# A four-layer graph network on one core: the maximum of layer 2 in one PSUM bank, narrower pieces for its count matrices, a bias row moved to layer 3, and more steps between the pieces of a node tile

## The chip, the cores and the metric

The kernel runs on one core of a Trainium2 chip. The metric is the time of one execution on the device in microseconds (us); less is better. The engines are named as the profile names them: PE (TensorE matmul), PEld (its weight loads), DVE (VectorE), ACT (ScalarE), POOL (GpSimd) and SP (SyncE, which here issues DMA transfers). PSUM is the memory that PE writes; its unit here is a bank of 128 partitions x 512 float32. SBUF is the working memory, DRAM the large one.

## What is computed

A graph of N = 6250 nodes (49 node tiles of 128) and E = 100000 edges, sorted by destination (782 edge tiles of 128). Node features are 256 wide, hidden ones 512 wide, float32. Low destinations have many more edges than high ones, because the destination is 6250 times the square of a uniform number.

```python
h = maximum(layernorm(x), 0)
h = h @ W1_self + mean_of_neighbours(h) @ W1_neigh + b1          # layer 1
hp = relu(h @ W2_pool + b2_pool)
h = h @ W2_self + max_of_neighbours(hp) @ W2_neigh + b2          # layer 2
h = ((sum_of_neighbours(h) + h) / (deg + 1)) @ W3_neigh + b3     # layer 3
h = h @ W4_self + mean_of_neighbours(h) @ W4_neigh + b4          # layer 4
out = x + h @ W_fc + b_fc
```

A node without edges has 0 for its maximum.

## The kernel before, in words

One function holds the fast path; a second, general path is run only if a flag (`bad`) says that the graph has not the expected form, which does not happen with these inputs. The kernel is written as loops that emit instructions for all engines; a scheduler then orders them on each engine by that order of emission and by what they depend on, and each engine runs its own instructions strictly in order. Work that is to lie beside a main loop is cut into generators (Python functions that `yield` between pieces); the main loop asks each for a piece at every step. So the number of `yield`s between two pieces sets how much of the main loop's work comes between them in the engines' queues.

**Sums over neighbours** (layers 1, 3 and 4) are done in two ways. For high destinations, gathered rows are multiplied on PE by one-hot matrices (`sums`, L382 on). For low destinations ("hubs", node tiles d below 18), a dense matrix A of edge counts is made per d (128 destinations by 49 x 128 sources) and multiplied on PE (`dense`, L469 on). Features go into these matmuls as three bf16 parts, high, middle and low (`parts`, L293 to L299: ACT copies the high part, DVE subtracts, ACT copies the middle one, DVE subtracts).

**Count matrices.** `build` (L309 on) makes A of tile d from windows of 8 destinations: 16 windows for each d. For each piece of a window ACT makes a one-hot of 128x128 in two steps (ht L319, hs L321), DVE one of 128x392 (hm L323: 49 source tiles x 8 destinations), PE multiplies them into a PSUM bank (pb L329), ACT reads that bank twice: once to find a count that is too large (many L337, with an accumulator, in `most`), once to copy it to A as fp8 (L339). SP stores A (tab_a) at the end of a d. A window of d = 8 and above has at most 256 edges, so two pieces. `Hub.advance` (L345 on) makes the one-hots `LOOK` = 4 pieces ahead of the matmul; ht has 3 buffers, hs and hm 7. Tiles d = 0 to 7 are made in layer 1, d = 8 to 17 during layer 2.

**Layer 2, the maximum** (main loop L1218 to L1292). The edges lie in six blocks of 52, 100, 220, 180, 130 and 100 tiles, each block one partition-major stretch of edges, taken from the last to the first. Each of the 782 steps is for one edge tile: POOL issues a gather of 128 rows of 2 KB (L1240) into a buffer of two steps (X2, 2 x 3 buffers), DVE takes the running maximum within a destination, `run = max(run * same, X)` (L1247), where `same` is 1 if this edge has the destination of the one before it on the partition, and 0 otherwise. For each pair of steps, one more instruction writes the maximum of both steps into the first row of the pair (L1283), and SP stores that (L1288). The running maximum goes to and fro between two PSUM banks (run0, run1 of the pool psr2).

**Beside the maximum** every step also advances: `products2` (weight products, first 64 steps), `hub` (count matrices of d = 8 to 17; d 8 to 15 by step 250, the rest after it, to step 682), `early` (below), the `carry` at the end of a block (L1113 to L1143: it joins the running maxima of the 128 partitions), and node tiles, `done2` (L1157 to L1196). `done2` of node tile d gathers the stored maxima (tot, L1149), joins them (L1164), transposes them on PE (L1168), copies them with ACT (hT L1170), multiplies with products of weights (L1173, L1176, L1179), adds the bias row prow with DVE (L1183), adds the result to layer 3's sum of that tile if d is below 16 (L1040), splits it in three parts and stores it (tab_r). From emission to end it takes about nine steps, and nothing but a count of tiles begun (49 in the steps from 112 to 762) sets when the next may start.

**Early products** (L1199 to L1215): for node tiles 6 to 37 layer 3's dense products start in layer 2, in batches of four source tiles: for each of the 16 destinations d, SP loads a piece of A (ae L1211), PE makes 3 matmuls for each source tile (pd L489), and the product is added to acc3[d] by DVE (`add3`, L1040) as soon as the last matmul has been emitted; the first addition of each d is a copy by ACT (L1043). Products use two PSUM banks (psd2). A share of 1/40 of the pieces left is emitted per step.

PSUM has eight banks of this kind; layer 2 has 3 for transposes and node tiles, 2 for early products, 1 for count matrices (psb2), 2 for the maximum.

**Prologue.** Edges of a window have to be found: `select`, `begins`, `row_begins`, `window_keys` (L656 to L770 or so) count for each window where it begins in the sorted list, in groups of 128 windows, 3 groups; `begins` gathers 128 rows of 782 destinations (drow L689, one buffer) and counts in them on DVE (L693).

## Time and profile before

| | |
|---|---|
| time, median of 3 runs | 3320.49 us (3316.07 to 3323.73) |
| the profiled execution: time | 3354.4 us |
| its span, first to last instruction | 3352.6 us |
| its mean granted TensorE clock | 0.885 |
| prologue and layer 1 | 0 to about 916 us |
| layer 2 | about 916 to 2345 us, of which the loop over edge tiles to about 2280 |
| layers 3 and 4 | about 2345 us to the end |

Durations below come from the profiled execution, which took 33.9 us longer than the median of the runs. A row of a group reads: line, engine, operation, output<-inputs with shapes, number of instructions, then busy us in all and mean ns of one, then idle time of that engine just before them with what ended it. A row of a view of waits reads: engine, what waited <- what it waited for, us in total, times, the longest. In a view by windows each engine has its busy us and (in brackets) the number of its instructions; then come the granted clock of TensorE, the share of the DMA engines that was busy, and the rate in GB/s.

### The profile page before, as it was taken

The page shows a single profiled execution, that of the slowest core. Times are in us where ns is not written, and L with a number is a line of the kernel's source. Part 1 is how long each engine was busy: PE and PEld are TensorE (multiplying, and loading weights), DVE is VectorE, ACT ScalarE, POOL GpSimd, SP SyncE. Part 2 cuts the span into 40 slices and gives each one's busy share as a digit, 9 for nine tenths or more (in the row PEclk, how much of TensorE's full clock was granted, in tenths as well). Part 3 has the DMA queues.
Part 4 walks back from the last instruction along what each step waited for, and adds up shares of the span by engine and source line. Part 5 has one row for each costly group of instructions (what it writes and reads, how often), then busy time and mean ns, then how long its engine had stood idle before and what let it go on. Part 6 is the DMA issues. An engine that isn't in the chain of part 4 may idle for free.

```text
span 3352.6 us, 39513 instructions
## 1 busy us (share of the span) xinstructions
PE 2515.0 (75%) x11395; PEld 1293.9 (39%) x11523; DVE 2178.8 (65%) x5588; ACT 993.2 (30%) x2703; POOL 1948.2 (58%) x2255
## 2 busy tenths in 40 slices
PE   4557888889776555588888923872889999888887
PEld 2134556556443222233333411331333333444444
DVE  7845555655378778677777886785456656355555
ACT  4845555553256787322111110000000001000000
POOL 4266656666455555555565666563666665566664
PEclk9678989999887676789989966986999999999999
DMA  5455656666688788788888888886999998666675
GB/s 175 150 150 150 171 168 178 180 189 181 193 276 260 251 266 280 257 282 270 277 282 277 285 283 263 268 280 208 366 325 328 340 323 298 214 197 198 202 205 170
DMA packets 350368, 806.06 MB, mean 240 GB/s; under 512 B 55694, under 2 KB 147318, under 8 KB 350108
## 3 DMA queue, kind: packets, MB, share of 16 engines
q0 software_dynamic: 146080, 513.65, 50.2%
q1 hardware_dynamic: 145976, 234.34, 19.2%
q10 hardware_dynamic: 58084, 55.44, 5.4%
q8 instruction: 93, 1.52, 0.2%
q14 instruction: 135, 1.11, 0.1%
HBM read 604.85 MB, written 199.17 MB: 240 GB/s over the span
## 4 chain that ended last, share of the span: by engine, by line
PE 55%; issue 13%; DVE 11%; ACT 7%; DMA 7%; another core or an unknown queue 5%; POOL 3%; ACTq 0%; DVEq 0%; POOLq 0%; SPq 0%
PE pd L489 15%; PE pg L433 10%; PE pd L484 5%; DVE run L1247 3%; PE pd L485 3%; PE pb L329 3%; PE pm_prf L1179 3%; PE pm_hp L928 3%; PE pm_hp L931 2%; PE pm_w L263 2%; PE pm_prf L1173 2%; PE pg L428 2%; DVE X L1283 2%; ACT hs L321 2%
## 5 line engine op out<-in xcount | busy, mean ns | idle before, releaser
L1240 POOL DMA_INDIRECT X<-rows,srcIf x782 | 755.3, 966 | 565.8 <-issue 212.5
L411 POOL DMA_INDIRECT ring<-tab_h,srcT x474 | 452.5, 955 | 280.7 <-issue 99.0
L433 PE MATMUL pg<-ring,hot 128*128 128x512 bf16 (+2 forms) x2431 | 532.3, 329 | 82.8 <-issue 34.4
L1247 DVE SCALAR_TENSOR_TENSOR run<-run,samef,X 128x512 f32<-128x512 f32 x758 | 571.6, 754 | 34.1 <-DMA X<-rows,srcIf 11.5
L462 DVE SCALAR_TENSOR_TENSOR acc<-pg,M,acc 128x256 f32<-128x256 f32 (+2 forms) x694 | 356.4, 538 | 150.8 <-PE pg L433 48.5
L411 POOL DMA_INDIRECT ring<-tab_r,srcE x342 | 332.9, 973 | 194.4 <-issue 80.4
L329 PE MATMUL pb<-hm,hs 128*128 128x392 bf16 x781 | 262.5, 380 | 223.2 <-ACT A L339 96.4
L489 PE MATMUL pd<-r,ae 128*128 128x512 bf16 x1494 | 368.9, 395 | 66.7 <-DVE acc L1040 41.1
L411 POOL DMA_INDIRECT ring<-tab_s,srcE x314 | 301.4, 960 | 187.9 <-PE pg L429 68.6
L321 ACT ACTIVATE hs<-ht,onef 128x128 bf16<-128x128 bf16 x781 | 293.5, 397 | 348.5 <-PE pb L329 128.1
L433 PEld LDWEIGHTS <-hot 128*128 128x128 bf16 x2448 | 245.8, 101 | 328.5 <-issue 183.9
L407 DVE TENSOR_SCALAR hot<-iota_bf,keyE 128x128 bf16<-128x128 bf16 x656 | 159.6, 272 | 260.5 <-PE pg L429 101.9
L484 PE MATMUL pd<-zt,ac 128*128 128x512 bf16 x835 | 300.0, 388 | 25.9 <-issue 23.7
L1283 DVE SCALAR_TENSOR_TENSOR X<-X,samef,run 128x512 f32<-128x512 f32 x379 | 279.6, 738 | 0.0
L485 PE MATMUL pd<-zt,ac 128*128 128x256 bf16 x882 | 245.1, 278 | 29.3 <-issue 26.8
L489 PEld LDWEIGHTS <-ae 128*128 128x128 fp8e4 x1536 | 155.2, 101 | 288.5 <-issue 141.9
L489 PE MATMUL pd<-zt,ac 128*128 128x512 bf16 x797 | 229.2, 386 | 24.0 <-issue 14.7
L407 DVE TENSOR_SCALAR hot<-iota_bf,keyT 128x128 bf16<-128x128 bf16 x474 | 119.9, 265 | 169.8 <-PE pb L329 51.5
L489 PE MATMUL pd<-Z,A 128*128 128x256 bf16 (+1 forms) x1176 | 195.2, 282 | 26.5 <-issue 10.1
L329 PEld LDWEIGHTS <-hs 128*128 128x128 bf16 x781 | 82.3, 106 | 286.3 <-issue 207.1
L1179 PE MATMUL pm_prf<-unf,hTf 128*128 128x512 f32 x392 | 189.0, 608 | 4.5 <-issue 4.4
L323 DVE TENSOR_SCALAR hm<-iota_w,mk 128x392 bf16<-128x392 f16 x461 | 150.0, 340 | 53.2 <-PE pb L329 23.9
(329 smaller groups left out, 3559.7 us busy)
## 6 DMA issues: line engine op xcount, KB each, us to landing
rows<-X SPq DMA_DIRECT2D x385, 256.0 KB
tab_r<-r SPq DMA_DIRECT2D x49, 384.0 KB
tab_a<-A SPq DMA_DIRECT2D x18, 784.0 KB
tab_t<-th SPq DMA_DIRECT2D x49, 256.0 KB
rows<-hpf SPq DMA_DIRECT2D x49, 256.0 KB
th<-tab_t ACTq DMA_DIRECT2D x49, 256.0 KB
X<-rows,srcIf POOLq DMA_INDIRECT x782
ac<-tab_a ACTq DMA_DIRECT2D x90, 112.0 KB
```

Of the source, the lines that this page charges most:

```text
L321: nc.scalar.activation(hots[0], t, AF.Relu, bias=one, scale=-1.0)
L329: nc.tensor.matmul(hold[0], hots[0], hots[1], start=(k == 0), stop=(k == k_of[w] - 1))
L411: nc.gpsimd.indirect_dma_start(out=ring[:, j % deep, :], out_offset=None, in_=table, in_offset=bass.IndirectOffsetOnAxis(ap=srcT[:, j - jb ...
L433: nc.tensor.matmul(pg[:, : F + c], hot[j], X[:, part * F : (part + 1) * F + c], start=(k == 0 and part == 2), stop=(k == n - 1 and part == 1),
L462: nc.vector.scalar_tensor_tensor(acc[d], half, m, acc[d], op0=ALU.mult, op1=ALU.add)
L484: nc.tensor.matmul(hold[0], a, z[:, : 2 * F], start=(s == ss[0]), stop=False)
L485: nc.tensor.matmul(hold[0][:, :F], a, z[:, 2 * F :], start=False, stop=(s == ss[-1]))
L489: nc.tensor.matmul(hold[0][:, : F + c], a, z[:, part * F : (part + 1) * F + c], start=(s == ss[0] and part == 2), stop=(s == ss[-1] and pa ...
L1179: nc.tensor.matmul(pm, hT[:, c, :], un[:, c, :], start=False, stop=(c == KH - 1))
L1240: nc.gpsimd.indirect_dma_start(out=X[:, k, :], out_offset=None, in_=tab_p, in_offset=bass.IndirectOffsetOnAxis(ap=srcI[:, t : t + 1], axis=0),
L1247: nc.vector.scalar_tensor_tensor(run, prev, same[:, t : t + 1], X[:, k, :], op0=ALU.mult, op1=ALU.max,)
L1283: nc.vector.scalar_tensor_tensor(X[:, 0, :], X[:, 1, :], same[:, t : t + 1], before, op0=ALU.mult, op1=ALU.max,)
```

## The change

1. Count matrices of d = 8 and above (new function `build_narrow`): windows of 4 destinations instead of 8 (`WIN2`), 32 for each d, and one piece for each (at most 128 edges). The number of matmuls and of hm stays at 320; hm and the matmul are 196 wide instead of 392. Two pieces share a PSUM bank, ACT copies both at once, and that copy is emitted one pair later (`copies`). hs is made for four pieces at a time (128x512). hm has 16 buffers, hs 5 of four pieces, and the look ahead is 12 pieces. There are two banks (psb2). The check of counts reads A in SBUF in four "looks" per d, at up to 128x1664, in place of one read of PSUM per window. A has two buffers.
2. The running maximum stays in one PSUM bank, in place: first `run` with the pair's first row, then the pair's maximum into that row of X from the second row and `run`, then `run` with the second row. Number and width of the instructions stay.
3. The bias row of layer 2 leaves `done2` (49 additions of 128x512 on DVE, L1183) and goes into `qrow`, which layer 3 adds anyway; this holds because layer 3 divides the sum of deg + 1 equal rows by deg + 1. ACT now copies the high part from PSUM, and the first subtraction and `add3` read PSUM.
4. `done2` has about 21 steps instead of nine: 6 instead of 4 before the maximum, one before and one after the transposed copy, three after the matmuls, two after the high part, two after the middle one. A tile starts 11 steps after the last at the earliest. `carry` and `node_rows` have more steps too; `carry` gathers before it transposes.
5. The sum of an early product is not emitted at its end but just before the last piece of the next product (`take_sums`). Early pieces go at 1/32 of what is left per step.
6. The prologue has 4 groups of windows instead of 3: one `select`, one `begins` (a gather into the one drow buffer, and a count on DVE) and one column in each of the small tiles more.

The diff, cut to its core:

```diff
-WIN = 8
+WIN, WIN2 = 8, 4
...
+    def build_narrow(d, keys, pool, psb, copies):
...
+            def hot(r=r, v=v):
+                i = v % 4
+                if i == 0:
+                    held["ht"] = pool.tile([P, 4, P], BF16, name="ht", bufs=2)
+                nc.scalar.activation(held["ht"][:, i, :], iota_b, AF.Abs, bias=sk[:, r : r + 1])
+                hm = pool.tile([P, NT * WIN2], BF16, name="hm", bufs=16)
+                nc.vector.tensor_scalar(hm, iota_w[:, : NT * WIN2], mk[:, r : r + 1], None,
+                                        op0=ALU.is_equal)
+                held["hm", v] = hm
+                if i == 3:
+                    hs = pool.tile([P, 4, P], BF16, name="hs", bufs=5)
+                    nc.scalar.activation(hs, held["ht"], AF.Relu, bias=one, scale=-1.0)
+                    held["hs", v // 4] = hs
...
+                nc.tensor.matmul(pb[:, i * NT : (i + 1) * NT, :].rearrange("p s c -> p (s c)"),
+                                 held["hs", v // 4][:, v % 4, :], held.pop(("hm", v)),
+                                 start=True, stop=True)
...
+                def look(n):
+                    s0, s1 = LOOKS[n]
+                    at = NW1 + len(LOOKS) * (d - H1) + n
+                    many = pool.tile([P, 13, P], BF16, name="many", bufs=1)
+                    nc.scalar.activation(many[:, : s1 - s0, :], A[:, s0:s1, :], AF.Relu,
+                                         bias=less, accum_out=most[:, at : at + 1])
+
+                if i == 1:
+                    for f in copies[:2]:
+                        f()
+                    del copies[:2]
+                    copies.insert(0, copy)
+                    if v == WT2 - 1:
+                        copies.extend(lambda n=n: look(n) for n in range(len(LOOKS)))
...
-        psb = late.enter_context(tc.tile_pool(name="psb2", bufs=1, space=PSUM))
+        psb = late.enter_context(tc.tile_pool(name="psb2", bufs=2, space=PSUM))
...
-            yield from bias_rows(psm, b3c, B4, qrow)
+            yield from bias_rows(psm, b3c, B4, qrow, b2r)
...
+            yield
+            yield
+            yield
+            r3 = early_pool[0].tile([P, 3 * FH], BF16, name="r3", bufs=2 * BATCH + 1)
+            hi, mid, lo = (r3[:, i * FH : (i + 1) * FH] for i in range(3))
+            nc.scalar.copy(hi, pm)
+            yield
+            yield
+            if d < H3:
+                add3(d, pm)
             pr = wk.tile([P, FH], F32, name="prf")
-            nc.vector.tensor_add(pr, pm, prow)
-            yield
-            if d < H3:
-                add3(d, pr)
-            r3 = early_pool[0].tile([P, 3 * FH], BF16, name="r3", bufs=2 * BATCH + 1)
-            parts(pr, FH, r3)
+            nc.vector.tensor_sub(pr, pm, hi)
+            yield
+            nc.scalar.copy(mid, pr)
+            yield
+            yield
+            nc.vector.tensor_sub(lo, pr, mid)
...
-                             lambda s: batch[s], FH, psd, lambda v, d=d: add3(d, v))
-                early.add([(load, work[0])] + work[1:])
+                             lambda s: batch[s], FH, psd, lambda v, d=d: summed.append((d, v)))
+
+                def then(w):
+                    take_sums()
+                    w()
+
+                early.add([(load, work[0])] + [lambda w=w, i=i: then(w) if i == len(work) - 2 else w()
+                                               for i, w in enumerate(work[1:])])
...
+            run = psr.tile([P, FH], F32, name="run")
...
+                    row, st = X[:, k, :], same[:, t : t + 1]
+                    if s0 + G2 >= tb:
+                        step(row, X[:, 0, :] if k else run, st, row)
+                        if k:
+                            stored(b, s0 // 2, X)
+                    elif k == 0 and s0:
+                        step(run, run, st, row)
+                    elif k:
+                        held = run if s0 else X[:, 0, :]
+                        if s0 == 0:
+                            step(run, held, st, row)
+                        step(X[:, 0, :], row, st, held)
+                        if s0:
+                            step(run, run, st, row)
+                        stored(b, s0 // 2, X[:, :1, :])
...
-                    early.advance(early.done + math.ceil(early.left() / 40))
+                    early.advance(early.done + math.ceil(early.left() / 32))
...
-                    if tiles and not ends and begun2 < NT * (at - FIRST_AT) / (T - 20 - FIRST_AT):
+                    if (tiles and not ends and at >= begun_at + 11
+                            and begun2 < NT * (at - FIRST_AT) / (T - 20 - FIRST_AT)):
+                        begun_at = at
```

188 lines of the change are left out of this document (104 added, 84 removed).

## The prediction

> **What bounds the kernel now.** I read the page's table of busy time first, then the windows by stage, then the waits of POOL and DVE inside layer 2, then the groups by line there.
>
> The page: span and busy time of each engine.
>
> ```profile
> span 3352.6 us, 39513 instructions
> PE 2515.0 (75%) x11395; PEld 1293.9 (39%) x11523; DVE 2178.8 (65%) x5588; ACT 993.2 (30%) x2703; POOL 1948.2 (58%) x2255
> ```
>
> No engine is full over the span, and the stages differ. Almost all of the change lies in layer 2, so the next view cuts that out (916 to 2345 us), then its stages, then one stretch of 20 us.
>
> ```profile
> core 0: us, PE busy (x) PEld busy (x) DVE busy (x) ACT busy (x) POOL busy (x), PEclk, DMA share, GB/s
> 916.00:2345.00 1429.00, 955.46 (x3174) 434.32 (x3216) 1097.03 (x2068) 470.04 (x1320) 814.12 (x845) 0.82 0.82 269
> 916.00:1060.00 144.00, 111.99 (x377) 59.83 (x376) 114.87 (x324) 77.98 (x221) 79.91 (x85) 0.93 0.85 277
> 1060.00:1460.00 400.00, 229.58 (x622) 97.45 (x624) 311.01 (x678) 271.48 (x826) 225.24 (x231) 0.72 0.81 264
> 1460.00:1970.00 510.00, 422.65 (x1534) 189.93 (x1561) 400.80 (x640) 98.81 (x239) 295.58 (x307) 0.92 0.85 277
> 1970.00:2280.00 310.00, 177.26 (x609) 80.40 (x620) 242.81 (x373) 19.95 (x33) 191.29 (x198) 0.79 0.85 274
> 2280.00:2345.00 65.00, 13.98 (x33) 6.72 (x35) 27.54 (x57) 1.82 (x3) 22.10 (x24) 0.58 0.55 185
> 1985.00:2005.00 20.00, 0.00 (x0) 0.00 (x0) 16.77 (x25) 0.00 (x0) 15.11 (x17) 0.50 0.94 311
> ```
>
> The loop over the 782 edge tiles runs from 916 to 2280, 1364 us, and a tail of 65 us follows. DVE works 1097.03 of 1429, so it is idle 332 us; by stage 29.1, 89.0, 109.2 and 67.2 us in the loop and 37.5 in the tail. The last row is a stretch where nothing runs but gathers and the maximum: 17 gathers in 20 us at 311 GB/s, DMA share 0.94. That is the most that this mix of transfers reaches here. Bytes of the loop: 144 x 277 + 400 x 264 + 510 x 277 + 310 x 274 = 372 MB. At 311 GB/s they take 1196 us: the loop can lose at most 1364 - 1196 = 168 us, whatever DVE does.
>
> Are the gathers late, or does DVE hold them up? The waits of POOL, which issues the gathers, in layer 2 (what was waited for, us in total, times, longest):
>
> ```profile
> POOL X L1240 <- DVE run L1247: 132.9, 60, 6.5
> POOL X L1240 <- DVE X L1283: 44.9, 22, 5.8
> POOL X L1240 <- DMA rows<-X: 40.7, 28, 9.5
> POOL X L1240 <- DVE hm L323: 35.5, 22, 7.9
> ```
>
> and the waits of DVE in the same window:
>
> ```profile
> DVE acc L1040 <- remote: 47.3, 14, 7.9
> DVE hm L323 <- remote: 29.6, 9, 8.8
> DVE prf L1183 <- remote: 27.8, 4, 11.0
> DVE hm L323 <- PE pb L329: 21.3, 22, 3.4
> ...
> DVE run L1247 <- DMA X<-rows,srcIf: 9.6, 13, 1.3
> ```
>
> DVE waits for gathered rows 9.6 us in all, POOL waits 132.9 + 44.9 + 35.5 = 213 us for slots that DVE frees. **DVE is the pace-maker.** It runs in order, so a hub piece (hm), an early sum (acc) or a node tile (prf) that waits for PE or ACT holds the maxima behind it. "remote" is a release whose sender the trace did not resolve; for these three consumers it can only be PE or what PE waits for.
>
> **The change part by part.** The groups of DVE in layer 2 by line (xcount, busy, mean ns, then idle ahead of them):
>
> ```profile
> L1247 DVE SCALAR_TENSOR_TENSOR run<-run,samef,X 128x512 f32<-128x512 f32 x755 | 569.3, 754 | 32.1 <-issue 9.6 <-DMA X<-rows,srcIf 9.6 <-DVE run L1247 2.4
> L1283 DVE SCALAR_TENSOR_TENSOR X<-X,samef,run 128x512 f32<-128x512 f32 x378 | 278.9, 738 | 0.0
> L323 DVE TENSOR_SCALAR hm<-iota_w,mkR 128x392 bf16<-128x392 f16 x313 | 100.7, 329 | 67.7 <-remote 29.6 <-PE pb L329 21.3 <-issue 10.0
> L1040 DVE TENSOR_TENSOR acc<-acc,pd 128x512 f32<-128x512 f32 x112 | 76.3, 681 | 66.4 <-remote 47.3 <-PE pd L489 16.5 <-issue 2.5
> L297 DVE TENSOR_TENSOR prf<-prf,r 128x512 f32<-128x512 f32 x49 | 33.8, 689 | 26.9 <-ACT r L296 15.9 <-ACT ht L319 7.7 <-ACT hs L321 3.1
> L1183 DVE TENSOR_TENSOR prf<-pm_prf,prowf 128x512 f32<-128x512 f32 x49 | 33.6, 686 | 59.9 <-remote 27.8 <-PE pm_prf L1179 13.1 <-issue 6.1
> L299 DVE TENSOR_TENSOR r<-prf,r 128x512 bf16<-128x512 f32 x49 | 33.6, 686 | 8.2 <-issue 7.1 <-ACT r L298 0.9
> ```
>
> those of ACT:
>
> ```profile
> L321 ACT ACTIVATE hs<-ht,onef 128x128 bf16<-128x128 bf16 x314 | 117.6, 402 | 183.1 <-PE pb L329 60.7 <-remote 48.6 <-PE pd L489 25.3
> ...
> L337 ACT ACTIVATE many<-pb,less 128x392 bf16<-128x392 f32 x159 | 93.1, 586 | 114.3 <-PE pb L329 62.9 <-issue 23.2 <-remote 20.4
> ...
> L337 ACT ACTIVATION_READ_ACCUMULATOR many<-pb,less 128x1 f32 x159 | 31.5, 198 | 0.0
> ...
> L296 ACT CAST r<-prf 128x512 bf16<-128x512 f32 x49 | 30.2, 615 | 162.5 <-DVE prf L1183 48.5 <-issue 45.4 <-DVE run L1247 35.0
> ```
>
> and one group of the whole page, of the same kind of instruction as hm:
>
> ```profile
> L407 DVE TENSOR_SCALAR hot<-iota_bf,keyT 128x128 bf16<-128x128 bf16 x474 | 119.9, 265 | 169.8 <-PE pb L329 51.5
> ```
>
> (1) Bias row. The 49 additions at L1183 go: 33.6 us of DVE. The bias joins a row that layer 3 adds in any case, so nothing comes back there.
>
> (2) Four-node pieces. There are still 320 hm, 196 wide instead of 392. It takes 265 ns at 128 columns and 329 at 392: 0.242 ns per column, so 265 + 68 x 0.242 = 281 ns. 320 x 48 ns = 15 us of DVE go. On ACT, hs falls from 320 of 402 ns to 80 of 128x512; the nearest row that wide is L296 with 615 ns: 129 becomes 49 us. PE's matmuls halve in width, which only frees PE.
>
> (3) The check (many) falls from 160 of 586 + 198 ns, 125 us of ACT, to 40 "looks" at up to 13 x 128 = 1664 columns. No row is that wide. From L321 (128 wide, 402) and L337 (392 wide, 586) comes 0.70 ns per column, so 402 + 1536 x 0.70 = 1.47 us, with the accumulator's read 1.67: 67 us. Bounds: nothing for a piece that ACT runs while DVE wants nothing of it, and 40 x 1.67 = 67 us if DVE waits behind every one; I take nothing, for ACT is busy 470 of 1429 us and falls to about 330. The Trainium skill's "ScalarE: Activation LUTs", section "What ACT_TABLE_LOAD costs", gives 280 ns + 0.833 ns per element for an ACTIVATE with a pointer bias: 1.67 us without the read, 75 us in all by its figures; the row at 392 (586 against 607) agrees within 4%. By it the sum stays the same.
>
> (4) One bank for the maximum. Instructions and widths of L1247 and L1283 stay; each maximum now reads and writes the same PSUM bank where before it went from one to the other. No row shows that. In SBUF, L1040 adds in place in 681 ns and L299 not in place in 686. I take nothing. Bounds: below, nothing, for each instruction does the same work; above, reading and writing that exclude each other and so double it, 0.754 us more for each of the 758 that do this. It is a rival below. The Trainium skill's "PSUM — Partial Sum Buffer", section "The four PSUM rules", speaks for caution: each bank is a separate physical SRAM, so a read and a write that lay in two memories now lie in one. It states no price, and no row here shows one. By it alone, the sum could lie anywhere in that rival's range.
>
> (5) Two banks for the hub, 16 hm buffers and a look of 12. This is what the freed bank is for. PE's own waits in layer 2:
>
> ```profile
> PE pb L329 <- ACT A L339: 89.7, 44, 9.0
> ...
> PE pd L489 <- DVE acc L1040: 41.1, 10, 8.7
> ```
>
> With one bank, PE waits for ACT's copy 89.7 us; hm buffers come free only when PE has read them, and DVE stands before hm 67.7 us. After the change, PE has a second bank and DVE runs twelve pieces ahead instead of four. I leave 20 us of the 67.7.
>
> (6) Steps between a node tile's pieces. DVE's idle time before L1183, L297 and L299 is 59.9 + 26.9 + 8.2 = 95 us: it is asked for the result as soon as PE or ACT is asked to make it. Now there are three steps between matmuls and the copy, two more before each subtraction, and tiles start at least 11 steps apart. A step is 1364/782 = 1.74 us, two steps 3.5, while one ACT copy takes 0.6. I leave 30. The cover is ACT's and PE's being on time; a stall of PE over about 5 us still shows.
>
> (7) Early sums are taken one product later, so PE is done long before: of 66.4 I leave 25. What is late next is PE, which may wait for DVE to free the product's bank (a rival). SP's loads of A pieces are issued where they were relative to their product; the maximum's store is issued one instruction earlier. Carry's extra steps spread the same instructions. Early pieces go at 1/32 instead of 1/40 of what is left per step; the total is unchanged.
>
> (8) The prologue makes one more group of window starts: one gather, one pass of 128x782 on DVE, one selection. Its gathers use one buffer and so come one after another:
>
> ```profile
> L689 POOL DMA_INDIRECT drow<-dflat,cI x3: 950/955/1102, 17.1 to 34.6; - x3
> ```
>
> Three from 17.1 to 34.6 is 8.75 us apart. Bounds: 0 (it is hidden behind other preparation) and 8.75; I take +5, as PE's first layer-1 work depends on other keys of that prologue only in part.
>
> **The sum.** DVE's work falls by 33.6 + 15 = 49 us, its waits by 48 + 65 + 41 = 154. DVE alone would then let the loop run in 1364 - 203 = 1161 us. That is under the 1196 that the bytes take at 311 GB/s, so from somewhere DMA takes over. I place the loop midway between its present 277 GB/s and the stretch's 311: 294 GB/s, 372/0.294 = 1265 us. So -99 in the loop, 0 in the tail (65 us, where only the last tile is unspread in both), +5 in the prologue: -94. The profiled execution took 3354.4 us, so 3260.4; it stood 33.9 over the median of the runs, 3320.49, and I subtract the same: **3226 us**, 2.8% faster.
>
> **The rivals.**
>
> A. Only the removed work counts. The stalls are PE's own ("remote" is over half of the waits of acc, and the clock falls to 0.72 in 1060 to 1460), and they move with the work. Then -49 + 5: 3320.5 - 44 = 3276 us. For it: three of the longest waits are over 7 us, longer than the added two or three steps. Against: hub and early sums get far more than three steps.
>
> B. DMA's ceiling is all that is left: -168 + 5, 3157 us. For it: DVE's own sum is below that. Against: all four stages of the loop have other transfers and pieces beside the gathers, and none exceeds 277.
>
> C. Nothing comes of it, the stalls go to other waits, 3314 to 3327. Against: 49 us of work on the pace-maker go in any case.
>
> D. **Slower:** PE waits for the late sums. There are 128 early products with two banks; the sum of one is issued only before the last piece of the next, behind what DVE has queued. PE's idle time while they run is (510 - 422.65) + (310 - 177.26) = 220 us, so it decides from 220/128 = 1.7 us per product; at 3 us, 128 x 3 - 220 = +164 of PE's own, less the 49 of DVE: 3320 + 115 = 3435. For it: PE already waits 41.1 us for exactly this add, 4 us a time. Against: DVE's work is 1097/782 = 1.4 us a step, so a sum issued a piece before it is needed is mostly done in time.
>
> E. **Slower:** the in-place maximum costs more. The forecast gain of 94 is used up at 94/758 = 0.124 us each, a mean of 878 ns at L1247. Doubled it is +572 - 94: 3798. For it only that no row shows it; against, in-place in SBUF is free.
>
> **How the numbers follow.** Forecast (3190 to 3260): 0.43. A (3260 to 3314): 0.24. B (3145 to 3190): 0.08. C: 0.05. D: 0.13, half of it between 3327 and 3350. E: 0.07. The range 3150 to 3350 leaves out half of D, E and the edge of B, some 0.15 to 0.18. A measurement of this kernel tells about 0.2%, 6.6 us, from no change. Faster by more than that: 0.43 + 0.24 + 0.08 = 0.75; within: 0.05; slower: 0.20.
>
> **What would show it.** Loop of layer 2 about 1265 us with 290 to 300 GB/s; DVE idle before hm near 20, before the tile's subtractions near 30, before the early sums near 25; L1247 still at 754 ns, hm at 281; no waits of pb for ACT's copy; waits of PE's products for acc not over about 100 us; ACT at about 330 us in layer 2; prologue later by 0 to 9 us. Wrong if L1247's mean rises, if "remote" waits of DVE remain over 80 us in all, if the loop's rate stays at 277 (then the removed waits have come back as others), or if PE's waits for acc grow to over 150 us.

## The result, and the profile after

The changed kernel takes 3314.47 us (median of 20 runs), the kernel before 3324.86 us (median of 20 runs beside them): a ratio of 0.9965, 95% interval 0.995 to 0.9979. So it is 0.35% faster, about 11 us where 94 were forecast. The profiled execution of the changed kernel took 3317.4 us, 3 us over its median; the one of before took 3354.4 us, some 30 over its own. The two profiles therefore differ by 37 us, more than the kernels do.

The page of the changed kernel, span and busy time:

```profile
span 3315.3 us, 39111 instructions
PE 2492.3 (75%) x11532; PEld 1288.2 (39%) x11532; DVE 2123.7 (64%) x5544; ACT 912.7 (28%) x2223; POOL 1938.3 (58%) x2257
```

The loop of layer 2, from its first maximum to its last, in one window of each kernel. Before, it lies from 909 to 2302 us. (The prediction took 916 to 2280, 1364 us, for it, 29 us too few; that the loop after is 1364 us long too is chance.)

```profile
core 0: us, PE busy (x) PEld busy (x) DVE busy (x) ACT busy (x) POOL busy (x), PEclk, DMA share, GB/s
909.00:2302.00 1393.00, 945.43 (x3152) 430.49 (x3195) 1092.60 (x2043) 471.38 (x1327) 808.57 (x839) 0.83 0.84 273
```

and after, with what lies ahead of the loop and behind it:

```profile
core 0: us, PE busy (x) PEld busy (x) DVE busy (x) ACT busy (x) POOL busy (x), PEclk, DMA share, GB/s
0.00:908.00 908.00, 681.71 (x3977) 434.09 (x3977) 537.04 (x2021) 480.37 (x1277) 504.73 (x760) 0.90 0.57 170
908.00:2272.00 1364.00, 927.90 (x3193) 427.42 (x3194) 1036.83 (x1993) 390.94 (x847) 798.51 (x838) 0.83 0.85 279
2272.00:3315.00 1043.00, 882.71 (x4363) 426.70 (x4363) 549.83 (x1530) 41.43 (x101) 635.05 (x659) 0.96 0.79 261
```

DVE's work fell by 1092.6 - 1036.8 = 56 us, as the prediction had it (49). The loop fell by 29 only, because DVE's idle time rose: 1393 - 1092.6 = 300 us before, 1364 - 1036.8 = 327 after. Where it stands, by DVE's groups in the loop after (last column: idle ahead of them):

```profile
L1317 DVE SCALAR_TENSOR_TENSOR run<-run,samef,X 128x512 f32<-128x512 f32 x758 | 572.5, 755 | 34.5 <-DMA X<-rows,srcIf 13.6 <-remote 9.2 <-issue 3.1
L1317 DVE SCALAR_TENSOR_TENSOR X<-X,samef,run 128x512 f32<-128x512 f32 x379 | 281.6, 743 | 31.5 <-remote 9.7 <-issue 7.3 <-DVE run L1317 3.3
L361 DVE TENSOR_SCALAR hm<-iota_w,mkR 128x196 bf16<-128x196 f16 x304 | 83.5, 279 | 0.5 <-PE pb L377 0.5
L1105 DVE TENSOR_TENSOR acc<-acc,pd 128x512 f32<-128x512 f32 x112 | 76.3, 681 | 92.4 <-remote 64.6 <-PE pd L548 16.5 <-issue 5.7
L1266 DVE TENSOR_TENSOR r<-prf,r 128x512 bf16<-128x512 f32 x48 | 32.9, 686 | 34.1 <-ACT r L1263 29.5 <-ACT ht L359 2.4 <-issue 2.1
L1261 DVE TENSOR_TENSOR prf<-pm_prf,r 128x512 f32<-128x512 f32 x48 | 32.8, 684 | 52.3 <-ACT r L1255 26.2 <-issue 26.1
L1105 DVE TENSOR_TENSOR acc<-acc,pm_prf 128x512 f32<-128x512 f32 x15 | 10.2, 682 | 19.3 <-ACT r L1255 17.4 <-issue 1.9
```

The wait ahead of hm is gone (67.7 to 0.5 us). The waits ahead of early sums and node tiles are not. Before, in the same loop window, the sums had 66.4 us as in the prediction's row, and the node tiles

```profile
L297 DVE TENSOR_TENSOR prf<-prf,r 128x512 f32<-128x512 f32 x48 | 33.1, 689 | 26.8 <-ACT r L296 15.9 <-ACT ht L319 7.7 <-ACT hs L321 3.1
L1183 DVE TENSOR_TENSOR prf<-pm_prf,prowf 128x512 f32<-128x512 f32 x48 | 32.9, 686 | 49.9 <-remote 27.8 <-issue 6.1 <-PE pb L329 5.0
L299 DVE TENSOR_TENSOR r<-prf,r 128x512 bf16<-128x512 f32 x48 | 32.9, 685 | 7.5 <-issue 7.1 <-ACT r L298 0.2
```

(the prediction's 59.9 for L1183 holds 10 us of the last tile, behind the loop). So it is 66.4 + 26.8 + 49.9 + 7.5 = 151 us before and 92.4 + 34.1 + 52.3 + 19.3 = 198 after. Another 31.5 us stand ahead of the pair's maximum, where there were none before. The waits for sums and tiles are few and long, as the view of DVE's waits shows (total, times, longest):

```profile
DVE acc L1105 <- remote: 64.6, 14, 14.1
DVE r L1266 <- ACT r L1263: 29.5, 5, 10.9
DVE prf L1261 <- ACT r L1255: 26.2, 5, 14.1
```

Here is the longest of them in the timeline (start, duration, engine, line):

```profile
1658.36 5.34 PE L548 MATMUL pd<-r,ae 128*128 128x512 bf16 x24
...
1660.67 0.75 DVE L1317 SCALAR_TENSOR_TENSOR run<-run,samef,X 128x512 f32<-128x512 f32 x1
...
1670.89 0.94 POOL L1215 DMA_INDIRECT tot<-rows,rows_of  x1 [0.30 <-issue]
...
1675.52 0.32 SPq L1294 DMA_DIRECT2D ae<-tab_a  x1
1675.53 0.69 DVE L1105 TENSOR_TENSOR acc<-acc,pd 128x512 f32<-128x512 f32 x1 [14.11 <-remote]
...
1676.27 1.01 PE L548 MATMUL pd<-r,ae 128*128 128x512 bf16 x2 [12.56 <-DVE acc L1105]
```

and what the engines do meanwhile, in three windows:

```profile
core 0: us, PE busy (x) PEld busy (x) DVE busy (x) ACT busy (x) POOL busy (x), PEclk, DMA share, GB/s
1664.00:1668.00 4.00, 0.00 (x0) 0.00 (x0) 0.00 (x0) 0.00 (x0) 3.09 (x4) 1.00 0.93 334
1668.00:1672.00 4.00, 0.00 (x0) 0.00 (x0) 0.00 (x0) 0.00 (x0) 2.92 (x4) 0.57 0.71 210
1672.00:1675.50 3.50, 0.00 (x0) 0.00 (x0) 0.00 (x0) 0.00 (x0) 0.00 (x0) 0.50 0.32 126
```

PE's 24 matmuls of two products are over at 1663.7 by their records, whose ends are modelled. The granted clock falls to 0.50, its value in the prediction's stretch from 1985 to 2005 us too, where PE has no work. DVE waits for the first of the two products until 1675.5. PE, ACT and DVE all stand still for 11.5 us. Only POOL goes on issuing gathers until its slots are full, the transfers run out, and then DVE is released. PE's semaphore update is recorded at 1675.51, and SP's load of a piece of A (`ae`), which waits for PE as well, is issued at 1675.52: two waiters are let go at once, so it is PE's release that is late and not DVE's start. No packet that loads instructions falls into the stall (the nearest start at 1654.9 and 1677.7). I call this a **late release**: work that is done by PE's records, whose release the waiting engine sees many us later. The 14.1 us ahead of L1261 look the same in the timeline: DVE waits for ACT's copy from 1378.9 to 1393.0, ACT for PE, and no matmul runs from 1381.1 on.

Not all waits end so. Of DVE's 17 waits over 5 us in this loop, the four of 13 us and more end 1 to 4 us after the last packet of a gather, but nine of the eleven under 10 us end while gathers still run.

### The profile page after: what moved, and what is told of

Its sections match the earlier page's. It is cut to its first block, busy times and chain, and to the rows that moved or that the text cites. A ratio compares the mean times of both kernels' runs of the same rounds, so it can differ in the third digit from the quotient of the medians.

```text
span 3315.3 us, 39111 instructions
## 1 busy us (share of the span) xinstructions
PE 2492.3 (75%) x11532; PEld 1288.2 (39%) x11532; DVE 2123.7 (64%) x5544; ACT 912.7 (28%) x2223; POOL 1938.3 (58%) x2257
## 5 line engine op out<-in xcount | busy, mean ns | idle before, releaser
L1336 POOL DMA_INDIRECT X<-rows,srcIf x782 | 746.3, 954 | 531.6 <-issue 229.2
L492 PE MATMUL pg<-ring,hot 128*128 128x259 bf16 (+1 forms) x2448 | 529.2, 328 | 73.2 <-issue 33.0
L548 PE MATMUL pd<-r,ae 128*128 128x512 bf16 x1536 | 376.9, 395 | 76.3 <-DVE acc L1105 43.2
L543 PE MATMUL pd<-zt,ac 128*128 128x512 bf16 x882 | 314.8, 387 | 26.6 <-issue 21.3
L1317 DVE SCALAR_TENSOR_TENSOR X<-X,samef,run 128x512 f32<-128x512 f32 x379 | 281.6, 743 | 31.5 <-remote 9.7
L548 PE MATMUL pd<-zt,ac 128*128 128x512 bf16 x816 | 229.3, 382 | 17.7 <-issue 12.5
L325 ACT ACTIVATE hs<-ht,onef 128x128 bf16<-128x128 bf16 x461 | 174.0, 393 | 169.1 <-PE pg L492 62.1
L333 PE MATMUL pb<-hm,hs 128*128 128x392 bf16 x461 | 158.6, 370 | 68.8 <-ACT hs L325 26.5
L323 ACT ACTIVATE ht<-iota_bf,sk 128x128 bf16<-128x128 bf16 x461 | 171.5, 395 | 19.8 <-DVE sk L831 13.1
```

Of the source, the lines that this page charges most:

```text
L323: nc.scalar.activation(t, iota_b, AF.Abs, bias=sk[:, r : r + 1])
L325: nc.scalar.activation(hots[0], t, AF.Relu, bias=one, scale=-1.0)
L492: nc.tensor.matmul(pg[:, : F + c], hot[j], X[:, part * F : (part + 1) * F + c], start=(k == 0 and part == 2), stop=(k == n - 1 and part == 1),
L543: nc.tensor.matmul(hold[0], a, z[:, : 2 * F], start=(s == ss[0]), stop=False)
L548: nc.tensor.matmul(hold[0][:, : F + c], a, z[:, part * F : (part + 1) * F + c], start=(s == ss[0] and part == 2), stop=(s == ss[-1] and pa ...
L1317: nc.vector.scalar_tensor_tensor(put, held, st, row, op0=ALU.mult, op1=ALU.max)
```

## The experiments

Two theories at the start. **Late releases**: they belong to the chip or to what goes on there, not to the kernel; DVE time that is freed is lost to more of this waiting. **Order**: the new order of pieces makes these waits. The expectations count late releases by the recorded semaphore updates of PE. In the profiles with long stalls only part of the updates is recorded (of DVE's 4952 there are 2484 in the first one), so those counts are upper bounds; what is concluded below rests on idle times and on the times of runs.

The kernels ran in five groups, each on another chip with runs of the kernel before beside them, and this turned out to be the main thing: on four of these chips the kernel before takes 2929 to 2932 us, on one 3365, near the 3325 of the measured runs.

**First group: before 2930.01 us.** The kernel before, unchanged.

> The kernel before, unchanged, for a second profile of it: the one shown took 33.9 us more than the median. Both theories: no difference in time, within 0.2%. If the first profile is an outlier through its stalls, DVE's idle time in the loop of layer 2 is some 20 to 30 us smaller here than its 300 us, and the loop nearer to 1365 us than to 1392.

Measured: 2928.73 us, ratio 1.0004 (0.9993 to 1.0015), on a chip on which the same program is 12% faster. The profile of it in the loop:

```profile
core 0: us, PE busy (x) PEld busy (x) DVE busy (x) ACT busy (x) POOL busy (x), PEclk, DMA share, GB/s
...
783.00:2021.00 1238.00, 915.49 (x3150) 423.52 (x3192) 1088.32 (x2043) 468.36 (x1324) 808.50 (x838) 0.85 0.92 307
```

DVE works as long as in the first profile (1088 and 1093 us) but is idle 150 us instead of 300. The loop starts at 783 us instead of 909, and what follows it takes 913 us instead of 1051: all stages are faster. DVE's instructions take the same time; what is missing is standing still. For instance DVE's wait ahead of the early sums is 6.9 us (66.4 in the first profile):

```profile
L1040 DVE TENSOR_TENSOR acc<-acc,pd 128x512 f32<-128x512 f32 x112 | 76.3, 681 | 6.9 <-PE pd L489 6.6
```

Only the bias row moved:

```diff
-            yield from bias_rows(psm, b3c, B4, qrow)
+            yield from bias_rows(psm, b3c, B4, qrow, b2r)
...
-            nc.vector.tensor_add(pr, pm, prow)
...
+            nc.scalar.copy(hi, pm)
...
+            nc.vector.tensor_sub(pr, pm, hi)
```

> The kernel before with the bias row moved to layer 3, and nothing else: 49 additions of 0.686 us, 33.6 us, leave DVE, which runs the loop. Theory 'late releases' (DVE's waits for PE are releases that come late while gathers stream; time that DVE gains becomes more of such waiting): 0 to 12 us faster, DVE's idle time in the loop up by 20 us or more. Rival 'order' (work that leaves DVE is gained in full, and what ate the gain in the changed kernel is the new order of pieces): 25 to 34 us faster, idle time as before.

Measured: 2909.85 us, ratio 0.9951 (0.9935 to 0.9967). That is 14 us by the ratio and 20 by the medians, of 33.6. In the two profiles DVE's idle time stays (150 and 146 us) and the loop ends 28 us earlier. The gain lies between what the two theories expected (0 to 12 and 25 to 34 us), and "late releases" is not put to the test, since this chip has none.

The changed kernel with its sums at the end of their product:

```diff
-                             lambda s: batch[s], FH, psd, lambda v, d=d: summed.append((d, v)))
+                             lambda s: batch[s], FH, psd, lambda v, d=d: add3(d, v))
```

> The changed kernel with the early sums added at the end of their product again, as before (the share of 1/32 stays). Theory 'late releases': the sum waits for PE wherever it stands, so within 10 us of the changed kernel, DVE's idle time before the sums about the 92 us that it shows there. Rival 'order': deferral is what makes PE wait for DVE and DVE for PE, so 20 us or more faster than the changed kernel. If deferral helps as I had meant, 20 us or more slower, with over 120 us of idle time before the sums.

Measured: 2845.20 us, ratio 0.9742 (0.9701 to 0.9784), with 8.3 us of idle time before the sums. There is no 92 us to win or lose on this chip. And with all the old steps:

```diff
-            for _ in range(6):
+            for _ in range(4):
...
-            yield
-            yield
-            yield
             r3 = early_pool[0].tile([P, 3 * FH], BF16, name="r3", bufs=2 * BATCH + 1)
...
-                    if (tiles and not ends and at >= begun_at + 11
+                    if (tiles and not ends
```

> The changed kernel with the old steps of a node tile, no distance of 11 steps between tiles, sums at the end of their product and 1/40 per step: what is left of the change is the single bank, the four-node pieces, the bias row and the steps of the carry. Theory 'late releases': within 10 us of the changed kernel, for the steps gain little where a release is late by 5 to 14 us. Rival 'order': 20 to 60 us faster than the changed kernel, near the forecast. Forecast of the prediction: 60 us or more slower than the changed kernel, since the steps were to save 65 + 41 us.

Measured: 2871.03 us, ratio 0.9806 (0.9788 to 0.9825): the new order of pieces (with the share of 1/32) is worth some 26 us against sums_at_once. Here the new order helps, so "order" falls for a chip of this kind; for the other kind see the fourth group.

**Second group: before 2929.85 us.** The changed kernel, unchanged.

> The changed kernel, unchanged, because the first four runs were on another chip than the two first profiles: there the kernel before takes 2930 us, and no release of PE comes later than 2.5 us after its matmul in layer 2, against 87 that do in the first profile of before. Theory 'late releases' (they belong to the chip, not to the kernel): on a chip that has none, the changed kernel is 70 to 95 us faster than the one before (2835 to 2860 beside 2930), DVE's idle time in the loop about 110 us; on a chip that has them, it is 0 to 25 us faster than before, with DVE idle over 280 us in the loop. Rival 'order' (the new order of pieces makes the waits that the first profile shows): no more than 0.5% faster on any chip, with 30 us or more of idle time before the sums.

Measured: 2851.46 us, ratio 0.9726 (0.9708 to 0.9744): 78 us, 2.7% faster, on a chip like the first group's. The loop and DVE's groups in it:

```profile
794.00:1943.00 1149.00, 887.21 (x3192) 412.80 (x3192) 1036.31 (x1993) 390.08 (x846) 799.94 (x838) 0.87 0.96 331
```

```profile
L361 DVE TENSOR_SCALAR hm<-iota_w,mkR 128x196 bf16<-128x196 f16 x304 | 84.5, 283 | 0.0
L1105 DVE TENSOR_TENSOR acc<-acc,pd 128x512 f32<-128x512 f32 x112 | 76.2, 680 | 6.5 <-PE pd L548 6.3
L1266 DVE TENSOR_TENSOR r<-prf,r 128x512 bf16<-128x512 f32 x48 | 32.8, 684 | 4.4 <-ACT r L1263 4.3
L1261 DVE TENSOR_TENSOR prf<-pm_prf,r 128x512 f32<-128x512 f32 x48 | 32.8, 683 | 2.4 <-ACT r L1255 2.4
L1105 DVE TENSOR_TENSOR acc<-acc,pm_prf 128x512 f32<-128x512 f32 x15 | 10.2, 682 | 4.6 <-ACT r L1255 4.6
```

The same program as in the result, with the same DVE work (1036.3 and 1036.8 us), has 18 us of waits ahead of sums and tiles here and 198 there. The loop is 1149 us long instead of 1364, and carries 331 GB/s. PE, ACT and DVE are idle together for 16 us of it here and for 129 us there, 113 of the 214 us by which DVE's idle time differs; in the rest PE or ACT works while DVE waits.

The old steps of a node tile alone (the diff of old_order without its sums and its share of 1/40):

> The changed kernel with the old steps of a node tile and no distance between tiles, but the sums still deferred. By the forecast, the steps save some 65 us of DVE's waits before the tile's subtractions. Theory 'late releases': on a chip without late releases the steps are worth about what the old order shows against the sums at once there, 2871 - 2845 = 26 us, so this kernel is 20 to 30 us slower than the changed one; on a chip with them, within 10 us. Rival 'order': faster than the changed kernel by 10 us or more on either.

Measured: 2875.46 us, ratio 0.9811 (0.979 to 0.9831): the steps are worth 24 us here. Idle time ahead of the second subtraction is 21.8 us with the old steps, 4.4 with the new ones; ahead of the first, 10.2 and 2.4.

Fewer buffers for gathered rows:

```diff
-        xmore = late.enter_context(tc.tile_pool(name="xrows2", bufs=3))
+        xmore = late.enter_context(tc.tile_pool(name="xrows2", bufs=2))
```

> The changed kernel with two buffers instead of three in the second pool of gathered rows, so 10 slots instead of 12, and about 8 in use between them. In the first profile of the changed kernel, gathers go on during a late release until the slots are full, and the release comes as the transfers end. Theory that a late release waits for the gathers: on a chip with late releases the longest ones are shorter, by two to four gathers of 1.25 us, and the loop is faster or as long. Rival, that gathers need their slots: slower by 10 us or more. On a chip without late releases: 0 to 15 us slower.

Measured: 3016.17 us, ratio 1.0301 (1.0276 to 1.0326). That is 165 us slower than with 12 slots, where 0 to 15 were expected without late releases: gathers need their slots. The wait of DVE for them is the row that grows, from 38.1 us with 12 slots to

```profile
DVE run L1317 <- DMA X<-rows,srcIf: 168.9, 96, 4.6
```

**Third group: before 2932.23 us.** The single bank in place and the second hub bank alone, in the kernel before:

```diff
-        psb = late.enter_context(tc.tile_pool(name="psb2", bufs=1, space=PSUM))
+        psb = late.enter_context(tc.tile_pool(name="psb2", bufs=2, space=PSUM))
...
+            run = psr.tile([P, FH], F32, name="run")
...
-                               else psr.tile([P, FH], F32, name=f"run{k}"))
```

> The kernel before with the maximum in one PSUM bank, in place, and the freed bank given to the count matrices; windows of 8, bias row, steps and sums as before. If the in-place maximum cost anything (rival E of the prediction), L1247's mean of 754 ns would rise here; expected: 750 to 758. On a chip without late releases: the second bank takes part of the 33 us that DVE waits before hm, so 10 to 30 us faster than before; the rest of the 40 us that old_order has over bias_only is then the four-node pieces (15 us of DVE's work and the deeper look). On a chip with late releases: within 10 us of before.

Measured: 2900.40 us, ratio 0.988 (0.9864 to 0.9897), 32 us from these two edits. Its groups of DVE show both halves of that step:

```profile
L1228 DVE SCALAR_TENSOR_TENSOR run<-run,samef,X 128x512 f32<-128x512 f32 x758 | 569.8, 752 | 17.6 <-DMA X<-rows,srcIf 14.0
...
L323 DVE TENSOR_SCALAR hm<-iota_w,mkR 128x392 bf16<-128x392 f16 x313 | 100.1, 324 | 5.1 <-PE pb L329 4.9
```

The maximum in place takes 752 ns, not more than between two banks (755 in before_again), and the wait ahead of hm falls from 33.0 to 5.1 us by the second bank, with windows of 8 and a look of 4.

More slots, with the sums at once:

```diff
-        xmore = late.enter_context(tc.tile_pool(name="xrows2", bufs=3))
+        xmore = late.enter_context(tc.tile_pool(name="xrows2", bufs=4))
...
-                X = (xmore if at // G2 % 2 else xpool).tile([P, G2, FH], F32, name="X2")
+                X = (xpool if at // G2 % 7 in (0, 2, 4) else xmore).tile([P, G2, FH], F32, name="X2")
```

> The changed kernel with its sums added at once (2845 us there), with four instead of three buffers in the second pool of gathered rows, taken so that 14 slots are in turn instead of 12 (hm has 15 buffers, not 16, for room). With 8 to 10 slots the loop took 164 us more and DVE waited 252 us before the maximum, with 12 it waits 62 to 69. If that curve goes on, another 10 to 25 us faster than the sums at once; if those waits are transfers at their limit, within 5 us. On a chip with late releases: gathers run on for two more slots in every one, so not faster than the changed kernel.

Measured: 2836.57 us, ratio 0.9673 (0.966 to 0.9686). With five buffers in a turn of eight:

> As slots14, with 16 slots, and for room 10 hm buffers, 3 of hs and a look of 6 pieces. If slots bound DVE's waits before the maximum: 5 to 15 us faster than slots14. If transfers bound them, or the shorter look costs: within 5 us of slots14 or slower.

Measured: 2840.68 us, ratio 0.9688 (0.9675 to 0.9701), no better: DVE's idle time before the two large groups of the maximum goes on falling (55 us with 12 slots in sums_at_once, 36 with 14, 17 with 16), but that before the node tiles' last subtraction rises from 6.6 to 10.1 and 22.6 us.

Every store of the maximum made twice:

```diff
-            nc.sync.dma_start(
-                runs[b][r0 * P : (r0 + n) * P, :].rearrange("(g p) f -> p g f", p=P), rows)
+            for _ in range(2):
+                nc.sync.dma_start(
+                    runs[b][r0 * P : (r0 + n) * P, :].rearrange("(g p) f -> p g f", p=P), rows)
```

> The changed kernel with every store of the maximum made twice, the same rows to the same place: some 100 MB more in the loop, on top of 372. Rival to 'the chip': PE's releases come late wherever transfers are dense, whatever the chip. Then on a chip that had no late releases there are 20 or more later than 2.5 us here. Theory that they belong to the chip: none or one, while the loop grows, as 472 MB at 311 to 340 GB/s take 1390 to 1520 us.

Measured: 3225.98 us, ratio 1.1003 (1.0983 to 1.1023), the loop 1520 us at 318 GB/s and DMA share 0.93, and not one late release in it: the wait ahead of the early sums is 2.8 us, that ahead of the two subtractions 0.1. Dense transfers alone do not make them on this chip.

**Fourth group: before 3365.18 us.** The changed kernel once more, on a chip like that of the result.

> The changed kernel once more, for another chip if one is given: two chips so far had no late release of PE, with 2930 us before. Theory 'late releases': where the kernel before takes about 2930 us, the changed one is 2.5 to 3.0% faster and has no release later than 2.5 us in layer 2; where it takes about 3320 us, the changed one is 0 to 0.7% faster and has 70 or more. Rival, that the time before has nothing to do with it: other pairings.

Measured: 3355.96 us, ratio 0.9973 (0.9956 to 0.999). The pairing holds: a long time before, a small gain, long stalls. There are two pairs of that kind now (this one and the result) and one of the other (after_again). DVE's waits in its loop, the two largest, and its groups for sums and tiles:

```profile
DVE acc L1105 <- remote: 61.5, 14, 14.0
DVE prf L1261 <- ACT r L1255: 56.2, 7, 14.9
```

```profile
L1105 DVE TENSOR_TENSOR acc<-acc,pd 128x512 f32<-128x512 f32 x112 | 76.2, 680 | 102.7 <-remote 61.5 <-PE pd L548 25.3 <-PE pm_prf L1244 10.3
L1266 DVE TENSOR_TENSOR r<-prf,r 128x512 bf16<-128x512 f32 x48 | 32.9, 685 | 41.8 <-ACT r L1263 32.4 <-issue 9.2
L1261 DVE TENSOR_TENSOR prf<-pm_prf,r 128x512 f32<-128x512 f32 x48 | 32.8, 683 | 64.8 <-ACT r L1255 56.2 <-issue 8.6
```

Eight slots on the same chip:

> The changed kernel with fewer slots again. Where PE's releases are late: if they come only once the gathers run dry, the longest (11 to 14 us with 12 slots) fall to under 10 us, DVE's idle time before sums and tiles falls by 40 us or more. If a late release has nothing to do with slots: lengths as before, and the loop as much slower as on the other chip, 150 us. Where there are none: 3% slower than before, as it was.

Measured: 3323.70 us, ratio 0.9888 (0.9857 to 0.9918): 32 us **faster** than the changed kernel beside it, where it was 165 us slower on the other chip. DVE's groups in its loop:

```profile
L1317 DVE SCALAR_TENSOR_TENSOR run<-run,samef,X 128x512 f32<-128x512 f32 x758 | 571.7, 754 | 137.3 <-DMA X<-rows,srcIf 111.0 <-issue 21.2 <-DVE hm L361 1.0
L1317 DVE SCALAR_TENSOR_TENSOR X<-X,samef,run 128x512 f32<-128x512 f32 x379 | 281.3, 742 | 77.8 <-issue 42.3 <-DMA X<-rows,srcIf 21.3 <-DVE hm L361 5.3
L361 DVE TENSOR_SCALAR hm<-iota_w,mkR 128x196 bf16<-128x196 f16 x304 | 82.7, 276 | 1.6 <-remote 1.6
L1105 DVE TENSOR_TENSOR acc<-acc,pd 128x512 f32<-128x512 f32 x112 | 75.9, 678 | 27.4 <-remote 15.3 <-PE pd L548 7.2 <-issue 3.7
L1266 DVE TENSOR_TENSOR r<-prf,r 128x512 bf16<-128x512 f32 x48 | 32.7, 681 | 0.1
L1261 DVE TENSOR_TENSOR prf<-pm_prf,r 128x512 f32<-128x512 f32 x48 | 32.7, 681 | 11.0 <-ACT r L1255 8.8 <-issue 2.2
```

Waits for slots grew as they did on the other chip (137.3 + 77.8 us; 153.3 + 82.2 there). But the waits ahead of early sums fell to 27.4 us (102.7 in after_third), and the two subtractions' to 11.1 (106.6); the longest for PE in the loop is 9.0 us (14.9). With fewer gathers that can run on, late releases are fewer and shorter, as the theory that they hang on the gathers had it. The loop tells it too: with 12 slots it takes 1394 us here and 1149 in after_again, with 8 slots 1346 and 1313, so 33 us apart instead of 245. This rests on one kernel with 8 slots on one such chip, and the stages ahead of the loop and behind it stay as far apart as they were.

The old order with the bias row back in layer 2:

```diff
-            nc.scalar.copy(hi, pm)
...
+            nc.vector.tensor_add(pr, pm, prow)
...
-            nc.vector.tensor_sub(pr, pm, hi)
...
+            parts(pr, FH, r3)
```

> The old order of steps and sums (old_order) with the bias row added in layer 2 again: so the single bank, the two hub banks with four-node pieces, and the longer prologue alone. By the runs so far, without late releases: old_order is 59 us faster than before, bias_only 20; if they add up, this is 35 to 45 us faster than before (2888 to 2897), with DVE's idle time before hm under 2 us. If the pieces are worth nothing beyond the second bank (two_hub_banks, 2900), it is 2900 to 2912, for the prologue's 11 us come on top. On a chip with late releases: within 15 us of before.

Measured: 3353.26 us, ratio 0.9979 (0.9952 to 1.0005): on this chip it is as fast as the full change (3355.96), which has 28 us less work on DVE and steps that were worth 24 us on the other chip. In the profiles the freed time stands as idle time: 308 us in the loop here, 356 in after_third (whose profile lies 15 us over its median, this one 4 under). The long stalls are there with the old order too: 72.1 us ahead of the early sums, 62.3 + 49.6 + 3.9 ahead of the node tiles. So the new order does not make them. Whether it adds some on such a chip, and so eats the bias row's gain, is not shown: the changed kernel with the old steps alone (old_order, tiles_close) was not run there. (How the gain splits without late releases was not seen with this kernel.)

**Fifth group: before 2928.53 us,** a chip without late releases again, so what the next four were to tell of late releases stays open. The kernel before with two buffers (the edit of eight_slots):

> The kernel before with two instead of three buffers in the second pool of gathered rows, 8 slots in effect. Where the kernel before takes 3320 to 3365 us: if a late release of PE lasts until the gathers run dry, it is 10 to 50 us faster than before, as the changed kernel was 32 us faster so; if the slots have to do with the changed kernel alone, slower by 20 us or more. Where it takes 2930 us: 30 to 120 us slower, since DVE waits for slots.

Measured: 3068.42 us, ratio 1.049 (1.047 to 1.051), 140 us slower, more than the 30 to 120 expected. The same five buffers in a turn of five, in the changed kernel:

```diff
+                X = (xpool if at // G2 % 5 in (0, 2, 4) else xmore).tile([P, G2, FH], F32, name="X2")
```

> The changed kernel with the same five buffers taken in a turn of five, so 10 slots in effect instead of 8. Where the time before is 3320 to 3365 us: between 8 slots (3324) and 12 (3356), or below both if the wait for slots (229 us with 8) falls faster than the late releases grow: 3290 to 3345. Where it is 2930 us: between 3016 (8) and 2851 (12), 2880 to 2950.

Measured: 2906.34 us, ratio 0.9918 (0.9899 to 0.9936). So on chips without late releases 8, 10 and 12 slots take 3016, 2906 and 2851 us. The edits of eight_slots and sums_at_once together:

> Eight slots and the early sums added at the end of their product. Where the time before is 3320 to 3365 us: late releases are waited for at the sum either way, so within 10 us of the changed kernel with eight slots (3324). If the deferral hides late releases, 15 us or more slower. Where it is 2930 us: within 10 us of 3016.

Measured: 3011.41 us, ratio 1.0289 (1.027 to 1.0307), 5 us under eight_slots. And slots14 again:

> The changed kernel with sums at once and 14 slots, the fastest where the time before is 2930 us (2837). Where it is 3320 to 3365 us: gathers go on for two more slots in every late release, so not faster than the changed kernel and up to 30 us slower, with the longest waits of DVE at 15 to 18 us; if late releases do not hang on the gathers, 5 to 20 us faster. Where it is 2930 us: as it was.

Measured: 2833.19 us, ratio 0.9681 (0.9666 to 0.9696). On two chips it is 3.2 to 3.3% faster than the kernel before, where the changed kernel, on another chip of that kind, is 2.7% faster; on the chip with late releases it was not tried.

## Why the prediction was wrong, point by point

**What bounds the kernel: right, and not far enough.** DVE is the busiest engine of the loop with 12 slots (74% of it in after_third, 90% in after_again). But half of the idle time that I read as the kernel's own waiting (300 us in the loop) was a property of where it ran: the same program has 150 us on another chip.

**(1) Bias row, (2) pieces on DVE: right.** 49 additions are gone, and hm takes 279 ns (281 forecast). DVE's work fell by 56 us (49 forecast).

**(3) ACT: too low, without effect.** hs takes 723 ns (615 forecast), a look 1604 (1470):

```profile
L392 ACT ACTIVATE many<-A,less 128x1536 bf16<-128x1536 fp8e4 (+1 forms) x40 | 64.2, 1604 | 2.3 <-PE pm_prf L1244 2.2
L366 ACT ACTIVATE hs<-ht,onef 128x512 bf16<-128x512 bf16 x80 | 57.8, 723 | 0.0
```

ACT works 391 us in the loop (330 forecast). Of the 61 us between, 14 come from the two sizes. Most of the rest is a slip of mine: I took times of groups, which overlap (584 us in all before, 458 after), from the 470 us of a window, which counts each moment once. No DVE wait of note goes back to a look. The Trainium skill's "ScalarE: Activation LUTs", section "What ACT_TABLE_LOAD costs", was nearer than my extrapolation: an estimate by its figures is 280 + 0.833 x 1568 = 1586 ns for the mean width, and 706 for hs.

**(4) One bank: right.** 755 ns, and 752 without the rest of the change; rival E falls. What I quoted from the Trainium skill's "PSUM — Partial Sum Buffer", section "The four PSUM rules", shows no price here.

**(5) Two banks: right.** 67.7 us of wait ahead of hm became 0.5 (20 forecast). Without late releases the second bank by itself takes 33.0 to 5.1 us (two_hub_banks).

**(6) Steps between a tile's pieces: the step that failed.** 95 us of waits (84 within the loop) were to become 30 and are 34.1 + 52.3 = 86, with 19 more ahead of the add to layer 3's sum. I wrote that the cover is PE's and ACT's being on time and that a stall over 5 us still shows, and then counted such stalls as if two steps, 3.5 us, would hide most of them. The stalls are 5 to 15 us long. Where there are none, the step does what I said, on less (4.4 + 2.4 us left of 36.6 in before_again; tiles_close: 24 us).

**(7) Sums one product later: failed in the same way.** 66.4 us were to become 25 and are 92.4, for a sum that is issued later still meets a product whose release is late (14.1 us in the timeline above). What the deferral is worth on such a chip was not measured. Where releases are on time there was nothing to gain: 6.9 us before, 6.5 after, and the kernel is as fast without the deferral (ratios 0.9742 and 0.9726 to the kernel before).

**(8) Prologue: outside its bounds both times, by little.** I took +5 us between 0 and 8.75. On the measured chip the loop starts 1 us earlier than in the first profile; between before_again and after_again it starts 11 us later (783 and 794).

**The sum and the ceiling.** I let DMA take over at 311 GB/s. Where releases are on time the loop carries 331 GB/s, slots14 336; the 20 us stretch was no ceiling. On the measured chip it never came to that, for the loop stayed at 279: DVE's waits were to fall by 154 us, and its idle time rose by 27. That my 94 us come near the 78 of after_again is luck. There before_again had 33.0 + 6.9 + 36.6 = 76 us of these waits, not 229, and the rate went past the 294 GB/s that I had set.

**The rivals.** The time lies at the lower edge of C (3314 to 3327, chance 0.05), and C's words fit: the stalls go to other waits. A had the mechanism: stalls are PE's own, they move with the work, and three steps do not cover them. It gave 3276 us; the measured gain is smaller still, since waiting grew by 27 us while work fell by 56. I had its evidence in the quoted waits (11.0, 8.8 and 7.9 us, "remote") and gave it 0.24. B does not arise, with the rate at 279 GB/s. D falls: PE's waits for the sums are 43.2 us after, 41.1 before. Two of the signs that I had named for being wrong came: the rate stayed, and DVE's "remote" waits are 97 us in the loop, over 80.

**What is shown, and what is open.** Shown: the same two programs gain 0.3% on one kind of chip and 2.7% on another. The waits on which (6) and (7) counted (151 us in the loop of the first profile, 44 in before_again) belong for the most part to the first kind, where PE's release comes late while gathers go on, and about half of DVE's additional idle time there is time in which PE, ACT and DVE all stand still. With 8 slots instead of 12 these waits shrink (one run). Dense transfers alone do not make them on a chip without them (stores_twice). Not shown: why releases come late there. A sender that the gathers hold up, or other work on that chip, would both look like this. So would the recording itself: the five profiles from such chips hold 22700 to 24200 semaphore updates, that of before_again 62668, and no run tells whether the missing records follow from the stalls or have to do with their cause.

## What to carry to other kernels

A wait of 5 to 15 us for an engine that finished long ago by its records need not come from the program's own order. Here spacing pieces by a few us did not hide such waits, and the time freed on the pace-maker came back as idle time. Look in the windows of the longest waits whether any engine works at all before counting them as gain. And measure a tuned kernel on more than one chip: the same change was 0.3% and 2.7%, and the number of slots that helped on one hurt on the other.

## What the runs showed of the hardware that I had not expected

The same program takes 2929 to 2932 us on four chips, and 3325 and 3365 in the two other groups of runs, with the same durations of DVE's instructions (hm 330 and 329 ns, the early sum 681 and 681, the maximum 755 and 754). On the latter, a release by PE can be seen 5 to 14 us after its matmul's record ends (the semaphore update at 1675.51 for products that ended at 1661.1 and 1663.7), and about half of DVE's semaphore updates are missing from the record (2484 of 4952 are there). An instruction on DVE that reads and writes the same PSUM bank of 128x512 takes 752 to 755 ns, as between two banks.
